# Later maxima and exps, an own copy of the second layer's first block, the values' bias with the attention's outputs, and another last step: one change with six parts to a two-layer kernel

## The chip, the cores and the metric

The kernel runs on one core of one Trainium2 chip. The metric is the time of one execution on the device in microseconds (us); the median of several executions counts. A core has a matrix engine (TensorE, in profiles PE, with weight loads as PEld), three engines for elementwise work (VectorE: DVE; ScalarE: ACT; GpSimd: POOL), and a sync engine (SP) that here only starts transfers. Each engine works through a queue of its own in the order written in the program, and waits on semaphores for the others. DMA transfers are started from the queues of SP, ACT and POOL.

## The reference

There are 8 batches of 512 rows and 512 features, all float32. Layer 0 is a graph attention: every row attends to the first 20 rows of its batch, in 16 heads and 2 directions, with a mask and an additive bias from 11 edge labels. Layer 1 is a self-attention over all 512 rows in 16 heads, with a layer norm before and after, scaled and shifted by gates computed from a condition vector.

```python
# layer 0; d = 0, 1 are the two directions of the edges
q_exp = where(x.sum(-1) == 0, 0, cond)                 # "live" rows
self_feat = concat([x, q_exp]) @ W_self.T + b_self
for d in range(2):
    aff = (self_feat @ Wq[d].T + bq[d]) . (self_feat[:, :20] @ Wk[d].T + bk[d]) / sqrt(32)
    aff = where(A[d].sum(-1) > 0, aff, -9e15) + A[d] @ w_bias + b_bias
    output += softmax(aff) @ self_feat[:, :20] @ Wout[d] + bout[d]
mid = x + relu(self_feat + output)
# layer 1
h = gamma * layernorm(mid) + beta                       # gamma, beta from cond
q, k, v = h @ Wqkv.T + bqkv
att = softmax(q . k) / sqrt(512)
h1 = (att @ v) @ Wp.T + bp + mid
out = gamma * layernorm(h1) + beta + h1
```

## The kernel before

**Start** (lines 169 to 385). SP loads, in this order, the near rows transposed and the first half of the self weights in four pairs of pieces (`vtk`, `ws`), batch 0 transposed (`vt`, four pieces), the condition's half of the self weights (`wc`), the near rows (`x_kv`, eight pieces) and batch 0 (`x`). PE computes the self features of the near rows (`psk`, 308), starts those of batch 0 (`psf`, 283), multiplies the condition by its weights (`pcw`, 253), and turns two sets of "live" flags (`pl`, 273) that DVE makes from row sums (`sums`, 265, needs `x`). Then come keys and output weights (`pk`, `pq`, `pw`). The values times output weights go to DRAM and are fetched per batch as block-diagonal tiles by `load_vo` (436 to 443, 20 transfers).

**Layer 0** (543 to 607) is a loop over 32 slots n = (b, c), a slot being 128 rows of batch b. It is a software pipeline written out by hand: slot n turns its own weights (`ptw`, 483), normalizes those of slot n+1 (`normalize0`: sum, reciprocal, POOL's multiply at 477), and computes the scores of slot n+2 (`scores0`, 454, with POOL's mask and bias at 460 and 461) and a quarter of the self features of the next batches (283 to 291). `exps0` (464 to 470) then subtracts the row's maximum (DVE 468, POOL 469) and takes the exp (ACT 470) of slot n+2. `result0` (488 to 497) sums self features and weighted values in `po`, DVE adds ReLU and x (496), and a store started from ACT's queue writes the block to `mid` in DRAM (497). Other work hangs at fixed slots: edge labels (`edges`, from 226), row sums of a later batch (`live_sums`), the second half of the keys (`keys(1, ..)`, n = 10 to 13), the gates' columns (`gates_t`, 515, n = 10). For layer 1, batch 0 is fetched back from `mid` at n = 23 (`fetch`, 97), its statistics are taken at n = 24, it is normed into `z` at n = 25 (108), turned at n = 26 and 27 (`turn`, 120), and the first queries, keys and values follow at n = 28 to 31. The same statistics and norm of batch 1 are at n = 29 and 30.

**Layer 1** (747 to 795) is a loop over 128 steps (b, group of 4 heads, 128 rows), again a pipeline by hand. In step n PE computes `scores(n+1)` (669), DVE the negated maxima (`tops`, 675), ACT the exps with their sums (681); `normalize` takes reciprocals on DVE (686) and scales on POOL (688); `turn_probs` transposes step n's probabilities (`pt`, 693) and ACT and DVE copy them (`et`, 695); `weigh` multiplies by the values (`pao`, 706), and ACT copies the result to `ao` (711 in the last batch, 713 before). Each step also holds half or all of one `Group` of four matmuls (133): queries, keys, values of the next batch, or the output projection (`ppj`) of the one before. A projection's `after` (643 to 646) adds the residual (645) and takes statistics (90 to 94); `finish` (648 to 656) applies norm and gates and stores the rows. The values' bias is multiplied by the output weights once and added to the output's bias (`value_bias`, 634 to 637, at step 2), since the probabilities of a row sum to a constant.

The last batch runs its steps in another order (664, row blocks outside), so that its own projections can start before all heads are done; `endings` (730) lists the projections of the last two batches, one half a step. In odd steps its `after` runs in the middle of the step, and a `finish` follows. Lines 796 to 802 are the tail: the last two `weigh`, and projection and `finish` of the last 128 rows.

Of the kernel before, what the change touches and what calls it, by code (L numbers as in the profile page):

```python
# [33 lines left out]


COLS = ["bk0", "bk1", "bq0", "bq1", "b_self", "b_q", "b_k", "b_v"]

# [5 lines left out]
@with_exitstack  # L43
def graph_then_self_attention(ctx: ExitStack, tc: tile.TileContext, x, x_t, near_t, cond_t, labels, w_self_t, wq, wk_t,
                              wout_t, wg_t, wb_t, wqkv_t, wp_t, cols, gate_vecs, rows, edge, out):
    nc = tc.nc
# [8 lines left out]
    make_identity(nc, ident)  # L55
    vec = const.tile([P, len(COLS), C], F32, name="vec")
    col = {name: vec[:, i, :] for i, name in enumerate(COLS)}
    edge_bc = const.tile([P, L + 1], F32, name="edge_bc")
    minus_half = const.tile([P, C], F32, name="minus_half")
# [40 lines left out]

    def norm_stats(b, c):
        statistics(XQ[b][:, c, :], f"{b}_{c}")

    def norm(b, c):
# [3 lines left out]
        nc.vector.tensor_scalar(Z[b][:, c, :], XQ[b][:, c, :], mv[:, 0:1], mv[:, 1:2], ALU.subtract, ALU.mult)  # L108

# [13 lines left out]
    class Group:  # L123
# [4 lines left out]

        def half(self, n):
            if n == 0:  # L130
                self.out = bank(self.name)
            for k in (2 * n, 2 * n + 1):
                nc.tensor.matmul(self.out, self.stationary(k), self.moving(k), start=(k == 0), stop=(k == C - 1))  # L133
            if n == 1:
                self.after(self.out)
# [17 lines left out]
    with ExitStack() as l0:  # L153
# [13 lines left out]


        vtk = three.tile([P, C, 2 * MH], F32, tag="t", name="vtk")
        ws = w0.tile([P, C, F], F32, name="ws")  # L170
        for k in range(C):
            nc.sync.dma_start(vtk[:, k, :], near_t[k * P:(k + 1) * P, :])
            nc.sync.dma_start(ws[:, k, :], w_self_t[k * P:(k + 1) * P, :])

        cond_sb = pro.tile([P, C, DH], F32, name="cond_sb")
        nc.vector.memset(cond_sb, 0.0)
        nc.scalar.dma_start(cond_sb[:, :, 0:B], blocks(cond_t))
        nc.scalar.dma_start(vec, cols.rearrange("p (k c) -> p k c", c=C))
        nc.scalar.dma_start(edge_bc, edge.partition_broadcast(P))

# [10 lines left out]
        def load_vt(b):  # L191
            VT[b] = turned.tile([P, C, N], F32, tag="turned", name=f"vt_{b}")
            for k in range(C) if b == 0 else (slice(0, C),):
                nc.sync.dma_start(VT[b][:, k], blocks(x_t[b])[:, k])

        load_vt(0)
        wc = weight("wc", w_self_t[F:2 * F, :])
        x_kv = wring.tile([MH, 2, F], F32, tag="w", name="x_kv")
        for i in range(2):
            for b in range(BH):  # L200
                nc.sync.dma_start(x_kv[NG * b:NG * (b + 1), i, :], x[BH * i + b, 0:NG, :])
        load_x(0)

        def room(name):
# [258 lines left out]

        def exps0(b, c):
            t = T[b, c]
            tv = t.rearrange("p h (d m) -> p (h d) m", d=2)
            top = three.tile([P, 2 * H, 1], F32, tag="top", name=f"top_{b}_{c}")
            nc.vector.tensor_reduce(top, tv, AX.X, ALU.max)  # L468
            nc.gpsimd.tensor_tensor(tv, tv, top.to_broadcast([P, 2 * H, NG]), ALU.subtract)  # L469
            nc.scalar.activation(tv, tv, AF.Exp)  # L470

        def normalize0(b, c):
            tv = T[b, c].rearrange("p h (d m) -> p (h d) m", d=2)
            den = three.tile([P, 2 * H, 1], F32, tag="den", name=f"den_{b}_{c}")
            nc.vector.tensor_reduce(den, tv, AX.X, ALU.add)  # L475
            nc.vector.reciprocal(den, den)  # L476
            nc.gpsimd.tensor_tensor(tv, tv, den.to_broadcast([P, 2 * H, NG]), ALU.mult)  # L477
# [55 lines left out]
        scores0(*slots[0])  # L533
        exps0(*slots[0])
        scores0(*slots[1])
        normalize0(*slots[0])
        exps0(*slots[1])
        for c in (0, 1):
# [4 lines left out]
        for n, (b, c) in enumerate(slots):  # L543
# [26 lines left out]
            if b + 1 + c // 2 < B:  # L570
                edges(b + 1 + c // 2, (c + 2) % 4)
# [57 lines left out]

    bv = w1.tile([P, C, P], F32, name="bv")  # L630

    def value_bias():

        pb = bank("pbv")
        for k in range(C):
            nc.tensor.matmul(pb, bv[:, k, :], wp[:, k, :], start=(k == 0), stop=(k == C - 1))
        nc.vector.tensor_tensor(bp_bc, pb, bp_bc, ALU.add)

# [10 lines left out]
    def finish(b, c):  # L649
# [47 lines left out]
    def weigh(n):  # L697
# [34 lines left out]

    with tc.manual_schedule():
        nc.sync.dma_start(bp_bc, rows[ROW_BP].partition_broadcast(P))
        fetch(2)
# [7 lines left out]
        for pair in range(2):  # L743
            normalize(0, pair)
        nc.vector.tensor_scalar(bv, col["b_v"].unsqueeze(2).to_broadcast([P, C, P]), att_scale, None, ALU.mult)

        for n, (b, g, c) in enumerate(steps):
# [53 lines left out]
        group.half(1)  # L801
        finish(B - 1, C - 1)

# [53 lines left out]
```

## Time and profile before

| | us |
|---|---|
| median of 3 runs (lowest, highest) | 1386.2 (1385.8, 1387.64) |
| the profiled execution | 1383.83 |
| its span, first to last instruction | 1382.0 |
| set-up, to the first slot of layer 0 | 80.4 |
| layer 0's slots, to layer 1 | 339.6 |
| layer 1 without its last batch | 859.0 |
| last batch and tail | 103.0 |

The mean clock granted to PE over the span is 0.995 of full speed. The four stretches are cut at 80.4, 420 and 1279 us of the span. All durations come from the one profiled execution; what an engine's "busy" leaves out are waits and the starting of transfers. A "releaser" is the instruction or transfer whose semaphore event ended an idle stretch. L477 stands for line 477 of the kernel before.

### The profile page before, as it was taken

How to read it: one execution, taken by the hardware profiler on the slowest of the kernel's cores; microseconds unless marked ns; L12 is line 12 of the kernel's file. 1: busy time of each engine (PE TensorE's matmuls, PEld its weight loads, DVE VectorE, ACT ScalarE, POOL GpSimd, SP SyncE). 2: the span in 40 equal slices, each digit the busy share in tenths (PEclk: the TensorE clock that was granted, in tenths of full speed). 3: DMA queues.
4: the chain of work that ended last, by engine and by line, in shares of the span. 5: the costliest groups of instructions: out<-in, count | busy, mean ns of one | idle time of the engine just before them, and what ended most of it. 6: DMA issues, size and time to landing. Idle time of an engine off the chain costs nothing.

```text
span 1382.0 us, 27718 instructions
## 1 busy us (share of the span) xinstructions
PE 1347.6 (98%) x10493; PEld 822.2 (59%) x10493; DVE 891.6 (65%) x1587; ACT 679.2 (49%) x1639; POOL 692.7 (50%) x807
## 2 busy tenths in 40 slices
PE   8999989999999999999999999999999999999997
PEld 5566666666665555655655555555556556555554
DVE  4566666666654456676577667657666765765786
ACT  1312122221125565655656666566566566566663
POOL 0255644556652345456355445545554553554655
PEclk9999999999999999999999999999999999999999
DMA  8624342344121000001001000100100010000001
GB/s 290 225 82 158 115 162 72 103 157 151 56 77 54 1 2 2 9 17 55 1 17 62 2 9 17 55 2 17 62 1 9 17 55 1 17 32 1 9 32 39
DMA packets 47043, 77.44 MB, mean 56 GB/s; under 512 B 10784, under 2 KB 15456, under 8 KB 46912
## 3 DMA queue, kind: packets, MB, share of 16 engines
q1 hardware_dynamic: 40976, 66.59, 14.2%
q10 hardware_dynamic: 5424, 8.43, 1.6%
q8 instruction: 85, 1.39, 0.4%
q0 software_dynamic: 512, 0.66, 0.2%
q14 instruction: 46, 0.38, 0.1%
HBM read 58.17 MB, written 17.49 MB: 55 GB/s over the span
## 4 chain that ended last, share of the span: by engine, by line
PE 78%; DVE 10%; POOL 6%; DMA 2%; issue 2%; SPq 1%; ACT 1%; ACTq 0%; POOLq 0%; DVEq 0%
PE pt L693 17%; PE pqk L133 15%; PE s L669 10%; PE pao L706 8%; PE pv L133 8%; PE ppj L133 8%; PE pss L454 4%; PE psf L283 3%; POOL t L460 2%; POOL t L461 2%; PE pw L423 1%; DVE top L468 1%; DVE sums L265 1%; DVE den L475 1%; PE pq L404 1%
## 5 line engine op out<-in xcount | busy, mean ns | idle before, releaser
L688 POOL TENSOR_SCALAR e<-e,den 128x512 f32<-128x512 f32 x512 | 374.6, 732 | 426.0 <-DVE den L686 387.1
L675 DVE TENSOR_REDUCE top<-s 128x2 f32<-128x1024 f32 x256 | 301.1, 1218 | 193.6 <-PE s L669 193.6
L681 ACT ACTIVATE e<-s,top 128x512 f32<-128x512 f32 x512 | 346.6, 701 | 11.9 <-DVE top L675 11.9
L693 PEld LDWEIGHTS pt<-ident,e 128*128 128x128 f32 x2048 | 229.4, 141 | 171.2 <-issue 90.0
L693 PE MATMUL pt<-ident,e 128*128 128x128 f32 x2048 | 274.1, 276 | 4.9 <-POOL e L688 4.6
L695 ACT COPY et<-pt 128x512 f32<-128x512 f32 x256 | 138.3, 589 | 235.0 <-PE pt L693 234.8
L133 PE MATMUL pqk<-ht,w 128*128 128x512 f32 x512 | 240.6, 593 | 0.0
L695 DVE COPY et<-pt 128x512 f32<-128x512 f32 x256 | 164.1, 683 | 0.0
L470 ACT ACTIVATE t<-t 128x640 f32<-128x640 f32 x32 | 23.6, 737 | 266.0 <-POOL t L469 266.0
L669 PE MATMUL s<-k,q 32*128 32x512 f32 x1024 | 147.4, 640 | 0.0
L454 PE MATMUL pss<-kq,sf 128*128 128x320 f32 x512 | 143.8, 434 | 0.0
L706 PEld LDWEIGHTS pao<-et,v 128*32 128x32 f32 x4096 | 107.7, 110 | 42.0 <-issue 40.8
L706 PE MATMUL pao<-et,v 128*32 128x128 f32 x4096 | 127.4, 274 | 0.6 <-ACT ao L711 0.4
L133 PEld LDWEIGHTS pqk<-ht,w 128*128 128x128 f32 x512 | 87.6, 190 | 62.5 <-issue 61.4
L133 PE MATMUL pv<-w,ht 128*128 128x512 f32 x256 | 120.9, 598 | 0.0
L133 PE MATMUL ppj<-w,ao 128*128 128x512 f32 x256 | 120.4, 593 | 0.0
L454 PEld LDWEIGHTS pss<-kq,sf 128*128 128x128 f32 x512 | 95.5, 191 | 36.5 <-issue 0.8
L283 PE MATMUL psf<-vt,ws 128*128 128x512 f32 x256 | 115.0, 593 | 0.0
L681 ACT ACTIVATION_READ_ACCUMULATOR e<-s,top 128x1 f32 x512 | 111.5, 218 | 0.0
L686 DVE RECIPROCAL den<-den 128x2 f32<-128x2 f32 x256 | 42.3, 165 | 84.2 <-ACT e L681 84.2
L477 POOL TENSOR_TENSOR t<-t,den 128x640 f32<-128x640 f32 x32 | 40.7, 1272 | 97.3 <-DVE den L476 87.0
L283 PEld LDWEIGHTS psf<-vt,ws 128*128 128x128 f32 x256 | 48.3, 190 | 50.7 <-issue 46.6
(186 smaller groups left out, 1351.9 us busy)
## 6 DMA issues: line engine op xcount, KB each, us to landing
x<-in_x SPq DMA_DIRECT2D x8, 1024.0 KB
mid<-x ACTq DMA_DIRECT2D x32, 256.0 KB
xq<-mid SPq DMA_DIRECT2D x8, 1024.0 KB
out<-o SPq DMA_DIRECT2D x32, 256.0 KB
vt<-in_x_t SPq DMA_DIRECT2D x7, 1024.0 KB
labels<-in_labels SPq DMA_DIRECT2D x16, 440.0 KB
wq<-in_wq SPq DMA_DIRECT2D x4, 1024.0 KB
gate<-gates SPq DMA_DIRECT2D x8, 512.0 KB
```

The costliest lines, as they stand in the source:

```text
L133: nc.tensor.matmul(self.out, self.stationary(k), self.moving(k), start=(k == 0), stop=(k == C - 1))
L283: nc.tensor.matmul(psf[f], ws[:, k, f * P:(f + 1) * P], VT[b][:, k, :], start=(k == 0), stop=(k == C - 1))
L454: nc.tensor.matmul(o, SF[b][:, k, cut], KQ[b][:, k, on], start=(k == 0), stop=(k == C - 1))
L477: nc.gpsimd.tensor_tensor(tv, tv, den.to_broadcast([P, 2 * H, NG]), ALU.mult)
L669: nc.tensor.matmul(S[n][j // 2][:, j % 2, :], Q[b, g][on, c * P:(c + 1) * P], K[b, g][on, :], start=True, stop=True)
L675: nc.vector.tensor_reduce(TOP[n][:, 2 * pair:2 * pair + 2], S[n][pair], AX.X, ALU.max, negate=True)
L681: nc.scalar.activation(e, S[n][j // 2][:, j % 2, :], AF.Exp, bias=TOP[n][:, j:j + 1], accum_out=DEN[n][:, j:j + 1])
L686: nc.vector.reciprocal(DEN[n][:, at], DEN[n][:, at])
L688: nc.gpsimd.tensor_scalar(E[n][j], E[n][j], DEN[n][:, j:j + 1], att_scale, ALU.mult, ALU.mult)
L693: nc.tensor.transpose(pt[:, k * P:(k + 1) * P], E[n][j][:, k * P:(k + 1) * P], ident)
L695: (nc.scalar.copy if j < 2 else nc.vector.tensor_copy)(et, pt.rearrange("p (k n) -> p k n", k=C))
L706: nc.tensor.matmul(PAO[b, g][DH * j:DH * (j + 1), at], V[b][:, k, DH * h:DH * (h + 1)], ET[n, j][:, k, :], start=(k == 0), stop=(k == C - 1))
```

## The change

Nothing in what is computed changes. The parts are:

- Layer 0: `exps0` is split. Maximum and subtraction (`less_top`) come after `result0` (in slots 26 to 29 still before it); the exp moves to the head of `normalize0`, in the next slot.
- The 32 stores to `mid` are started from SP's queue, in order with its loads, and no longer from ACT's.
- Start: `vtk` comes as one transfer from ACT's queue, `vt` of batch 0 in two, `x_kv` in one and after `x`; condition and edge weights come packed with the bias columns in one tile. Three matmuls on zeros stand ahead of PE's first work. `cond_r` is copied ahead of the sums of `x_kv`.
- Layer 1's first batch is normed from a copy of its own (`early`), loaded at n = 9; its statistics are spread over n = 15 to 18, its norm over 22 and 23; it is turned at n = 24 and 25, and its first groups are at n = 26, 27, 29 and 30. The last of the second layer's weights is loaded at n = 24 (before 20). Statistics and norm of batch 1 are one slot later, at 30 and 31.
- `value_bias` goes. ACT adds the scaled bias when it copies `pao` to `ao`.
- Last batch: `after` of a projection stands behind both reciprocals of the step; `finish` is in even steps. In the tail both `weigh` come first, and `finish_last` does the last 128 rows with two banks of 256 columns, statistics by halves, a side branch on POOL (`rest`) and two stores.

```diff
         vtk = three.tile([P, C, 2 * MH], F32, tag="t", name="vtk")
         ws = w0.tile([P, C, F], F32, name="ws")
+        nc.scalar.dma_start(vtk, near_t.rearrange("p (c m) -> p c m", c=C))
         for k in range(C):
-            nc.sync.dma_start(vtk[:, k, :], near_t[k * P:(k + 1) * P, :])
             nc.sync.dma_start(ws[:, k, :], w_self_t[k * P:(k + 1) * P, :])
-        cond_sb = pro.tile([P, C, DH], F32, name="cond_sb")
-        nc.vector.memset(cond_sb, 0.0)
-        nc.scalar.dma_start(cond_sb[:, :, 0:B], blocks(cond_t))
-        nc.scalar.dma_start(vec, cols.rearrange("p (k c) -> p k c", c=C))
-        nc.scalar.dma_start(edge_bc, edge.partition_broadcast(P))
+        nc.scalar.dma_start(vec, cols)
+        zeros = two.tile([P, N], F32, tag="live", name="zeros")[:, 0:2 * P]
+        nc.vector.memset(zeros, 0.0)
+        none = bank("none")
+        for i in range(3):
+            nc.tensor.matmul(none[:, 0:2 * P], zeros[:, 0:P], zeros, start=True, stop=True)
...
             VT[b] = turned.tile([P, C, N], F32, tag="turned", name=f"vt_{b}")
-            for k in range(C) if b == 0 else (slice(0, C),):
-                nc.sync.dma_start(VT[b][:, k], blocks(x_t[b])[:, k])
+            for cut in (slice(0, 2), slice(2, C)) if b == 0 else (slice(0, C),):
+                nc.sync.dma_start(VT[b][:, cut], blocks(x_t[b])[:, cut])
...
         x_kv = wring.tile([MH, 2, F], F32, tag="w", name="x_kv")
-        for i in range(2):
-            for b in range(BH):
-                nc.sync.dma_start(x_kv[NG * b:NG * (b + 1), i, :], x[BH * i + b, 0:NG, :])
         load_x(0)
+        nc.sync.dma_start(x_kv, near.rearrange("i m f -> m i f"))
...
         cond_r = two.tile([P, KB, P], F32, tag="wt", name="cond_r")[:, 0, :]
+        nc.vector.tensor_copy(cond_r, pcw[:, 2 * MH:2 * MH + P])
         nc.vector.tensor_reduce(sums_kv, x_kv, AX.X, ALU.add)
         nc.vector.tensor_scalar(sums_kv, sums_kv, 0.0, None, ALU.not_equal)
-        nc.vector.tensor_copy(cond_r, pcw[:, 2 * MH:2 * MH + P])
         live_sums(0)
...
-        def exps0(b, c):
+        def less_top(b, c):
             t = T[b, c]
...
             nc.gpsimd.tensor_tensor(tv, tv, top.to_broadcast([P, 2 * H, NG]), ALU.subtract)
-            nc.scalar.activation(tv, tv, AF.Exp)
         def normalize0(b, c):
+            nc.scalar.activation(T[b, c], T[b, c], AF.Exp)
             tv = T[b, c].rearrange("p h (d m) -> p (h d) m", d=2)
...
             nc.vector.scalar_tensor_tensor(X[b][:, c, :], po, 0.0, X[b][:, c, :], ALU.max, ALU.add)
-            nc.scalar.dma_start(mid[b, c * P:(c + 1) * P, :], X[b][:, c, :])
+            nc.sync.dma_start(mid[b, c * P:(c + 1) * P, :], X[b][:, c, :])
...
                 scores0(*slots[n + 2])
-            for i in range(2):
-                if i == 0 and b + 1 + c // 2 < B:
-                    self_feat(b + 1 + c // 2, ((c + 2) % 4,))
-                if i == 0 and n + 2 < len(slots):
-                    exps0(*slots[n + 2])
+            if b + 1 + c // 2 < B:
+                self_feat(b + 1 + c // 2, ((c + 2) % 4,))
+            if 26 <= n < len(slots) - 2:
+                less_top(*slots[n + 2])
             if c == 1 and b + 2 < B:
...
                 keys(1, n - 10, 0)
-            if n in (26, 27):
-                for f in (2 * (n - 26), 2 * (n - 26) + 1):
+            if n in (24, 25):
+                for f in (2 * (n - 24), 2 * (n - 24) + 1):
                     turn(0, f)
-            for i in {28: (0,), 29: (1,), 30: (2,), 31: (3,)}.get(n, ()):
+            for i in {26: (0,), 27: (1,), 29: (2,), 30: (3,)}.get(n, ()):
                 group = q_or_k(0, i, 0) if i < 2 else value(0, i - 2)
...
             result0(b, c)
+            if n < 26:
+                less_top(*slots[n + 2])
             if b + 1 + c // 2 < B:
...
-            if 17 <= n < 21:
-                W1.append(weight(f"w1_{n - 17}", (*(wqkv_t[i] for i in range(3)), wp_t)[n - 17]))
+            if n in (17, 18, 19, 24):
+                i = min(n - 17, 3)
+                W1.append(weight(f"w1_{i}", (*(wqkv_t[i] for i in range(3)), wp_t)[i]))
             if n in (23, 28):
                 fetch((n - 23) // 5)
-            if n == 24:
-                for i in range(C):
-                    norm_stats(0, i)
-            if n == 25:
-                for i in range(C):
-                    norm(0, i)
-            if n == 29:
+            if n == 9:
+                early = weight("early", mid[0])
+            if 15 <= n < 19:
+                norm_stats(0, n - 15, early)
+            for i in {22: (0, 1), 23: (2, 3)}.get(n, ()):
+                norm(0, i, early)
+            if n == 30:
                 for i in range(C):
                     norm_stats(1, i)
-            if n == 30:
+            if n == 31:
                 for i in range(C):
...
-    bv = w1.tile([P, C, P], F32, name="bv")
-    def value_bias():
-        pb = bank("pbv")
-        for k in range(C):
-            nc.tensor.matmul(pb, bv[:, k, :], wp[:, k, :], start=(k == 0), stop=(k == C - 1))
-        nc.vector.tensor_tensor(bp_bc, pb, bp_bc, ALU.add)
+    bv = w1.tile([P, C], F32, name="bv")
...
         nc.sync.dma_start(out[b, c * P:(c + 1) * P, :], o)
+    def finish_last():
+        b, c = B - 1, C - 1
+        h1, gate = XQ[b][:, c, :], GATE[b]
+        st = small.tile([P, 2, 6], F32, tag="st2", bufs=1, name="st_last")
+        mv = small.tile([P, 2], F32, tag="mv", name="mv_last")
+        o, rest = (op.tile([P, F], F32, tag="o", name=name) for name in ("o_last", "rest"))
+        out_p = [bank(f"ppj_last_{i}") for i in range(2)]
+        for i in range(2):
+            on = slice(i * F // 2, (i + 1) * F // 2)
+            for k in range(C):
+                nc.tensor.matmul(out_p[i][:, 0:F // 2], AO[b, k][:, c * P:(c + 1) * P], wp[:, k, on], start=(k == 0), stop=(k == C - 1))
+        for i in range(2):
+            on = slice(i * F // 2, (i + 1) * F // 2)
+            nc.vector.tensor_tensor(h1[:, on], out_p[i][:, 0:F // 2], h1[:, on], ALU.add)
+            nc.vector.bn_stats(st[:, i, :], h1[:, on])
+            nc.gpsimd.tensor_tensor(rest[:, on], h1[:, on], gate[:, 1, on], ALU.add)
+        nc.vector.bn_aggr(mv, st)
+        nc.vector.tensor_scalar(mv[:, 1:2], mv[:, 1:2], EPS, None, ALU.add)
+        nc.gpsimd.tensor_tensor(mv[:, 1:2], mv[:, 1:2], minus_half[:, 0:1], ALU.pow)
+        nc.vector.scalar_tensor_tensor(o, h1, mv[:, 0:1], gate[:, 0, :], ALU.subtract, ALU.mult)
+        for i in range(2):
+            on = slice(i * F // 2, (i + 1) * F // 2)
+            nc.vector.scalar_tensor_tensor(o[:, on], o[:, on], mv[:, 1:2], rest[:, on], ALU.mult, ALU.add)
+            (nc.scalar if i else nc.sync).dma_start(out[b, c * P:(c + 1) * P, on], o[:, on])
...
         if last:
-            nc.scalar.copy(AO[b, g][:, at], PAO[b, g][:, at])
+            nc.scalar.activation(AO[b, g][:, at], PAO[b, g][:, at], AF.Identity, bias=bv[:, g:g + 1])
         elif c == C - 1:
-            nc.scalar.copy(AO[b, g], PAO[b, g])
+            nc.scalar.activation(AO[b, g], PAO[b, g], AF.Identity, bias=bv[:, g:g + 1])
...
                 group.half(0)
-            elif b == B - 1:
-                ending[at // 2 - 1].half(at % 2)
+            elif b == B - 1 and more:
+                ending[at // 2 - 1].half(at % 2, take=False)
             if more:
...
                 finish(b - 1, (at - 3) // 2)
-            if b == B - 1 and at > 4 and at % 2:
-                finish(*endings[(at - 5) // 2])
+            if b == B - 1 and at > 2 and at % 2 and more:
+                ending[at // 2 - 1].after(ending[at // 2 - 1].out)
+            if b == B - 1 and at >= 4 and at % 2 == 0:
+                finish(*endings[at // 2 - 2])
             if group:
...
                 fetch(b + 2)
-            if n == 2:
-                value_bias()
             first = 0 if b == B - 1 else 10
...
                 bias(b, at - first)
+        ending[-1].half(1)
         weigh(len(steps) - 2)
+        weigh(len(steps) - 1)
         finish(*endings[-1])
-        weigh(len(steps) - 1)
-        group = project(B - 1, C - 1)
-        group.half(0)
-        group.half(1)
-        finish(B - 1, C - 1)
+        finish_last()
```

More of the change, by code (lines that the diff above doesn't have):

```diff
@@ L43, in graph_then_self_attention @@
 @with_exitstack
-def graph_then_self_attention(ctx: ExitStack, tc: tile.TileContext, x, x_t, near_t, cond_t, labels, w_self_t, wq, wk_t,
-                              wout_t, wg_t, wb_t, wqkv_t, wp_t, cols, gate_vecs, rows, edge, out):
+def graph_then_self_attention(ctx: ExitStack, tc: tile.TileContext, x, x_t, near, near_t, labels, w_self_t, wq, wk_t,
+                              wout_t, wg_t, wb_t, wqkv_t, wp_t, cols, gate_vecs, rows, out):
     nc = tc.nc
@@ L55, in graph_then_self_attention @@
     make_identity(nc, ident)
-    vec = const.tile([P, len(COLS), C], F32, name="vec")
-    col = {name: vec[:, i, :] for i, name in enumerate(COLS)}
-    edge_bc = const.tile([P, L + 1], F32, name="edge_bc")
+    nv = len(COLS) * C
+    vec = const.tile([P, nv + C * DH + L + 1], F32, name="vec")
+    col = {name: vec[:, i * C:(i + 1) * C] for i, name in enumerate(COLS)}
+    cond_sb = vec[:, nv:nv + C * DH].rearrange("p (c r) -> p c r", c=C)
+    edge_bc = vec[:, nv + C * DH:]
     minus_half = const.tile([P, C], F32, name="minus_half")
@@ L99, in fetch, with norm_stats, norm @@
         nc.sync.dma_start(XQ[b], blocks(mid[b]))
-    def norm_stats(b, c):
-        statistics(XQ[b][:, c, :], f"{b}_{c}")
-    def norm(b, c):
+    def norm_stats(b, c, src=None):
+        statistics((src or XQ[b])[:, c, :], f"{b}_{c}")
+    def norm(b, c, src=None):
         if c == 0:
@@ L107, in norm @@
         mv = STATS[f"{b}_{c}"]
-        nc.vector.tensor_scalar(Z[b][:, c, :], XQ[b][:, c, :], mv[:, 0:1], mv[:, 1:2], ALU.subtract, ALU.mult)
+        nc.vector.tensor_scalar(Z[b][:, c, :], (src or XQ[b])[:, c, :], mv[:, 0:1], mv[:, 1:2], ALU.subtract, ALU.mult)
     def bias(b, c):
@@ L127, in __init__, with half @@
             self.name, self.stationary, self.moving, self.after = name, stationary, moving, after
-        def half(self, n):
+        def half(self, n, take=True):
             if n == 0:
@@ L133, in half @@
                 nc.tensor.matmul(self.out, self.stationary(k), self.moving(k), start=(k == 0), stop=(k == C - 1))
-            if n == 1:
+            if n == 1 and take:
                 self.after(self.out)
@@ L533, in graph_then_self_attention @@
         scores0(*slots[0])
-        exps0(*slots[0])
+        less_top(*slots[0])
         scores0(*slots[1])
         normalize0(*slots[0])
-        exps0(*slots[1])
+        less_top(*slots[1])
         for c in (0, 1):
@@ L733, in graph_then_self_attention @@
     with tc.manual_schedule():
+        nc.vector.tensor_scalar(bv, col["b_v"], att_scale, None, ALU.mult)
         nc.sync.dma_start(bp_bc, rows[ROW_BP].partition_broadcast(P))
@@ L744, in graph_then_self_attention @@
             normalize(0, pair)
-        nc.vector.tensor_scalar(bv, col["b_v"].unsqueeze(2).to_broadcast([P, C, P]), att_scale, None, ALU.mult)
         for n, (b, g, c) in enumerate(steps):
@@ L826 @@
         gate_vecs[:, :B, i, :] = a[f"L1_cond_{name}"].reshape(4, 1, P)
+    cond = np.zeros((P, C, DH), np.float32)
+    cond[:, :, :B] = a["cond_1024"].reshape(B, C, P).transpose(2, 1, 0)
+    edge = np.tile(np.concatenate([a["L0_cond_w_bias"], a["L0_cond_b_bias"].reshape(1)]), (P, 1))
     arrays = {
@@ L829 @@
         "x_t": a["x"].transpose(0, 2, 1),
-        "near_t": a["x"][:, :NG].transpose(2, 0, 1).reshape(F, B * NG),
-        "cond_t": a["cond_1024"].T,
+        "near": a["x"][:, :NG].reshape(2, MH, F),
+        "near_t": a["x"][:, :NG].transpose(2, 0, 1).reshape(C, P, B * NG).transpose(1, 0, 2).reshape(P, C * B * NG),
         "labels": np.stack([adj[:, :, :NG], adj[:, :NG].transpose(0, 2, 1, 3)], axis=2).reshape(B, N, D2 * L),
@@ L840 @@
         "wp_t": a["L1_cond_Wp"].T,
-        "cols": np.concatenate([columns(vectors[name]) for name in COLS], axis=1),
+        "cols": np.concatenate([columns(vectors[name]) for name in COLS] + [cond.reshape(P, C * DH), edge], axis=1),
         "gate_vecs": gate_vecs.reshape(P, len(GATE_VECS), P),
         "rows": np.concatenate([a["L1_cond_bp"][None], a["L0_cond_bout"]], axis=0),
-        "edge": np.concatenate([a["L0_cond_w_bias"], a["L0_cond_b_bias"].reshape(1)]),
     }
```

## The prediction

> **What bounds it now.** I read the page's first section, then idle TensorE (PE) time by releaser (the waits view), then stretches (windows), then groups, the chain and a few timelines.
>
> ```profile
> PE   1347.6 (98%) x10493; PEld 822.2 (59%) x10493; DVE 891.6 (65%) x1587; ACT 679.2 (49%) x1639; POOL 692.7 (50%) x807
> 0.00:80.40 80.40, 73.88 (x523) 46.32 (x524) 37.76 (x100) 17.74 (x55) 20.86 (x32) 1.00 0.72 240
> 80.40:420.00 339.60, 325.52 (x1691) 221.36 (x1689) 212.71 (x429) 77.06 (x140) 185.09 (x144) 0.98 0.33 111
> 420.00:1279.00 859.00, 859.00 (x7376) 500.49 (x7376) 564.30 (x931) 528.86 (x1295) 426.53 (x559) 1.00 0.06 21
> 1279.00:1382.00 103.00, 89.16 (x906) 53.99 (x904) 76.83 (x129) 55.58 (x149) 60.24 (x74) 0.98 0.08 27
> ```
>
> The rows are set-up, layer 0's 32 slots, layer 1 without its last batch, and the last batch with the tail; columns: length, busy PE, PEld, DVE, ACT, POOL, clock. PE is the bound. From 420 to 1279 it never pauses, so there only removed PE work counts. Elsewhere it is idle 6.5 + 14.1 + 13.8 = 34.4 us, and some busy time is half-clock time. The idle time by cause:
>
> ```profile
> PE pt L693 <- POOL e L688: 4.6, 11, 0.5
> PE ptw L483 <- POOL t L477: 4.2, 4, 2.5
> PE pq L404 <- ACT gates_t L515: 4.2, 1, 4.2
> PE pz L120 <- DVE z L108: 2.5, 2, 2.2
> PE pq L404 <- ACT live L275: 1.5, 1, 1.5
> PE pl L273 <- DVE sfk L346: 1.3, 1, 1.3
> PE pcw L253 <- DMA wc<-in_w_self_t: 0.7, 1, 0.7
> ```
>
> (waiter, releaser: total, times, longest.) Each is a neighbour's queue order, not a lack of engine time. Timings below of single waits are the timeline's.
>
> **Layer 0, exps later.**
>
> ```profile
> L470 ACT ACTIVATE t<-t 128x640 f32<-128x640 f32 x32 | 23.6, 737 | 266.0 <-POOL t L469 266.0
> L477 POOL TENSOR_TENSOR t<-t,den 128x640 f32<-128x640 f32 x32 | 40.7, 1272 | 97.3 <-DVE den L476 87.0
> ```
>
> ACT stands 266 us in front of the exp, waiting for POOL's subtraction, with its copies of keys, gates and weights behind it. After the change the exp heads the next slot, its input ready one slot earlier. ACT's order becomes wt, exp, sf; DVE's x precedes the maximum, which idles 71.6 us on POOL today. No operation is added. Slots take 9.84 us (10.28 at c=1) without stalls; I charge the excess to its place:
> - n=5, 7, 9: .88 + .68 + .18; I take back 1.3.
> - n=10 to 13: 4.19 at the gates, then .4 + .4, then 1.46, plus a half-clock stretch of 3.41 us, which does half its work and so costs 1.7: 8.1. I keep .4 per slot, as key copies still fill these: 6.4 back.
> - n=25 to 27: .93, 2.18 + .33 and .11 + .59 of idle, 1.7 of half clock and about .5 of modelled ends: 6.3. Here also the early copy acts: z is made at n=22 and 23, two slots before its turn. The four statistics (.68+.18+.15 = 1.0 us DVE each) spread over n=15–18. 5.8 back.
> - n=30, 31: 2.49 + .4 idle, 1.7 of half clock: 4.6. DVE's 4.0 us of norm_stats(1) no longer stand ahead of den(31). But subtraction, exp .74, den 1.16 and multiply 1.27 for the last slot end about 6.6 us into slot 30, PE wants them at 5.5: 1.1 stays; the wt copy of .68, bare in slot 31, loses .4. 3.1 back.
>
> DVE at n=16 carries about 10.0 us for 9.84 (statistics, live sums of 2.2): I charge 1.0. Layer 0: 15.6 back; 10 if the new order stalls as often as half of the old, 18 if nothing stalls.
>
> The half-clock price is where rule and row differ. The Trainium skill, TensorE: Matmul & The Clock Gate, Why this matters for your kernels, asks for no idle gaps over about 3 us, since one idle window drops the clock. By that rule only the 4.19 gap costs clock, and the changes at n=26 and n=31 return 3.4 us less. The row speaks otherwise:
>
> ```profile
> 395.00:420.00 25.00, 22.51 (x93) 14.11 (x91) 12.64 (x27) 5.56 (x9) 11.18 (x11) 0.93 0.16 61
> ```
>
> After only 2.49 us of idle the matmuls from 412.69 to 416.11 ran at half rate; the same followed 2.18 + .33, while 1.46 and 1.27 cost no clock. I take the row.
>
> **mid on SP's queue.** 32 stores at .33 us of issue leave ACT, 10.6 us, none on the path. On SP they wait in order for x. Past them are moved: vo (20 issues) and labels behind mid(b,1), q_row behind mid(b,2), load_x behind mid(b,3), the next vt behind mid(b,0). load_x waited for that store already, vt and q_row are needed a slot or more later: nothing. vo and labels are the rival below. My value: 20 issues x .36 = 7.2, labels landing 3.7 later, so about 2.3 us into slot (b,3), against 5.7 before, since the 12 to 14 us that vo takes now include a wait for ACT's mid store. Zero cost; no gain counted.
>
> **Start.** x before x_kv, eight x_kv issues (8.29 us of SP) become one, constants in one DMA. x lands at 21.3 now and starts the chain sums 2.30, sfk, pl. Some 4.3 MB precede or are x; at the 320 to 400 GB/s of the DMA row from 10 us on it lands near 15. So .70 and 1.27 go. vtk as one 320 KB DMA beside ws may start PE .6 later. No row shows the three dummy matmuls: by psk's half-clock pace (.267 for 160 columns) 6 passes of 256 take 2.6 us. The same skill page and section ask for 4 us of continuous work before full speed, so by it 2.6 us and a gap bring nothing. The rows show full speed only at 9.92, 5.5 us after PE's first matmul, and all changes of clock on one grid of 3.41 us; work ahead of 4.41 can save one step, 1.7 us, or nothing (below nothing only by the .6). I take 1.3: together 3.3, range 1.4 to 4.
>
> **value_bias.**
>
> ```profile
> 450.63 3.43 PE pbv L636 x8
> ```
>
> The chain shows it with PE full: 3.43 goes, for certain. The bias on AO (28 + 16 ACT operations) makes 586 ns into about 688, the row of L141, same shape with a bias: +.10 each. ACT is busy 529 of 859, waits 35 us for pao; hidden. Uncovered, 28 x .10 = 2.9. w1_3 at n=24 is wanted 150 us later.
>
> **Last batch.** A pair of steps takes 12.87 us (1305.37 to 1318.24) for 11.38 of PE work; over 1293 to 1358 PE loses 8.3. The cause, from a timeline of an odd step:
>
> ```profile
> 1315.32 0.69 DVE L645 TENSOR_TENSOR xq<-ppj,xq 128x512 f32<-128x512 f32 x1 [0.74 <-PE ppj L133]
> 1316.05 0.69 DVE L90 BATCH_NORM_STATS2 st_h<-xq 128x6 f32<-128x512 f32 x1
> 1317.07 0.15 DVE L686 RECIPROCAL den<-den 128x2 f32<-128x2 f32 x1
> 1317.88 1.81 POOL L688 TENSOR_SCALAR e<-e,den 128x512 f32<-128x512 f32 x2
> 1318.62 0.55 PE L693 MATMUL pt<-ident,e 128*128 128x128 f32 x3 [0.38 <-POOL e L688]
> ```
>
> Addition and statistics (.69+.69+.18+.15 = 1.75 with gaps) stand before the reciprocal; POOL and PE wait for it. Moved behind both reciprocals, they leave the path, but DVE is then the loop: tops 2.35, reciprocals to about 3.0, et copies 1.28, second reciprocal .15, then 1.75 or finish's 1.5: 6.15 a step with gaps against PE's 5.69. Over 12 steps .46 each is 5.5, less 1.0 of slack: 4.5 lost instead of 8.3. 3.8 back; 0 if DVE's loop is as long as now, 7 if it overlaps fully, −3 if the longer-held ppj bank blocks the scores.
>
> **Tail.** From the last ppj (1373.6) addition, statistics, pow, two passes, POOL's gate and a DMA of 3.3 us run in line to 1382.0. Halves let .36 + .36 of DVE lie under PE, POOL's final 1.26 becomes a side branch, one pass lies under pow (1.0), the last pass and DMA are halved: about 2.3. The earlier last finish takes .74 passes and L655 out of the way: .8. 3.1, range 2 to 4.
>
> **Sum.** 15.6 + 3.3 + 3.4 + 3.8 + 3.1 = 29.2. The profiled execution took 1383.8 (span 1382.0 and 1.8 around it), 2.4 below the median of 1386.2. So span 1352.8, that execution 1354.6, median **1357**.
>
> **Rivals.**
> - Slower: labels. If vo needs its 14 us also behind mid(b,1), labels land 8.7 us into slot (b,3). DVE stands before edges, with t, den and x behind; POOL's multiply comes late, PE idles some 3.65 us and pays 1.7 of half clock: 5.3 for each of 6 batches, 32 in all: 1389. It decides from a landing about 5.1 us into the slot. For: DVE already waits 5.6 us for labels in four batches. Against: the cause of the long vo is gone. Chance .07, .02 of it for half of the batches.
> - Last batch: DVE becomes the bound at today's rate, 3.8 fewer: 1361. For: 6.15 above is near today's 6.43. Chance .16.
> - The start keeps its slow clock and late x, and layer 0 keeps its stalls in slots 30 and 31: 2 to 3 each: about 1363. Against: both have the order changed at their cause. Chance .13.
> - Better: stalls go with no rest, −5: 1352. It is in the forecast's case, which has .64.
>
> **Numbers.** Forecast's own range 1352 to 1361. 1350 to 1366 takes in the second and third rival and leaves the first, both misses together, and more than full gains. About 0.2% (2.8 us) is what a measurement tells from no change: faster .93, same .02, slower .05.
>
> **What would show it.** Right: the ACT idle behind L469 falls from 266 us to some tens; no clock drop after 100 us; no gates_t, z or live waits of PE; pbv absent; last-batch pairs near 12.3 us; PE busy about 1338 (1347.6 less 3.4 and 6.4 of half clock). Wrong: a PE wait through DVE edges for labels; dips of the clock at n=12 to 14, 26 or 31; xq statistics still ahead of PE's pt; PE start later than 5 us.

## The result and the profile after

The median fell from 1386.0 to 1360.9 us (4 runs each, 1360.13 to 1364.07 after), ratio 0.9823, interval 0.9804 to 0.9842. Forecast: 1357, range 1350 to 1366. The profiled execution after took 1364.07 (span 1362.3), the slowest of its four; that of before 1383.83, one of the fastest. So the two traces differ by 19.7 of span, the medians by 25.1; what is known of the difference is told below. First idle PE time after, by releaser:

```profile
PE ptw L486 <- POOL t L480: 3.1, 5, 1.7
PE pv L136 <- DVE x L499: 2.1, 1, 2.1
PE pq L407 <- DVE x L499: 1.6, 4, 0.4
...
PE pss L457 <- DVE kq L414: 1.0, 1, 1.0
PE pt L718 <- POOL e L713: 0.9, 2, 0.4
```

The waits for gates_t, live, z, sfk and wc are gone; `pt` waits 0.9 instead of 4.6. New are `pv` behind DVE's x, at the entry of layer 1, and `pss` behind a key copy. The exp's group shows the cause removed:

```profile
L475 ACT ACTIVATE t<-t 128x640 f32<-128x640 f32 x32 | 23.6, 737 | 78.1 <-POOL t L472 78.1
```

78 us of waiting instead of 266. Of the signs that the prediction named for being right, two did not come. PE is busy 1344.2 us and not about 1338, and the clock dropped after 100 us, at slot 31 (0.86 in the second row, 0.93 before):

```profile
PE 1344.2 (99%) x10499; PEld 823.7 (60%) x10499; DVE 907.2 (67%) x1589; ACT 687.5 (50%) x1639; POOL 692.2 (51%) x808
395.00:420.00 25.00, 20.73 (x82) 11.32 (x81) 12.69 (x28) 6.76 (x15) 8.28 (x11) 0.86 0.29 105
```

The stretches of the two traces, cut at the first instruction of the same work (gain in us):

| stretch | predicted | traces |
|---|---|---|
| start, to the first slot | 3.3 | 80.44 to 78.64: 1.8 |
| slots 0 to 13 | 7.7 | 163.38 to 154.77: 8.6 |
| slots 14 to 20 | −1.0 | 69.38 to 72.35: −3.0 |
| slot 21 to layer 1's first `pt` | 8.9 | 116.02 to 113.28: 2.7 |
| bias matmuls | 3.4 | 3.43 |
| last batch, to the last step's `pt` | 3.8 | 4.5 |
| tail | 3.1 | 1.6 |

The entry of layer 1 after, from the timeline (start, length, engine, line):

```profile
407.21 1.22 DVE L700 TENSOR_REDUCE top<-s 128x2 f32<-128x1024 f32 x1 [2.85 <-PE s L694]
408.35 0.14 DVE L96 TENSOR_SCALAR mv<-mv 128x1 f32<-128x1 f32 x1
408.41 0.68 DVE L499 SCALAR_TENSOR_TENSOR x<-po,x 128x512 f32<-128x512 f32 x1
```

```profile
401.45 0.76 PE L486 MATMUL ptw<-ident,t 128*128 128x128 f32 x5 [1.72 <-POOL t L480]
402.05 0.60 PE L496 MATMUL po<-ident,sf 128*128 128x128 f32 x4
403.05 2.50 PE L498 MATMUL po<-vo,wt 128*128 128x128 f32 x10 [0.40 <-ACT wt L488]
405.49 1.60 PE L694 MATMUL s<-k,q 32*128 32x512 f32 x8
409.24 4.94 PE L136 MATMUL pv<-w,ht 128*128 128x512 f32 x7 [2.15 <-DVE x L499]
```

In the instruction stream DVE has layer 1's first maximum (`top`) ahead of x of slot 31, though the source has it behind: where the two hand-ordered regions meet, their instructions were merged. DVE stands in front of `top` until the scores end, x waits behind it, and PE's `pv` waits for the bank that x frees. The pauses of 1.72 + 0.40 and of 2.15 us each brought a stretch of 3413 ns at half clock (403.06 and 409.89): `po` takes 2.50 instead of 1.28.

### The profile page after: what moved, and what is told of

It reads as the page before. It is cut to its first block, busy times and chain, and to the rows that moved or that the text cites. A ratio compares the mean times of both kernels' runs of the same rounds, so it can differ in the third digit from the quotient of the medians.

```text
span 1362.3 us, 27708 instructions
## 1 busy us (share of the span) xinstructions
PE 1344.2 (99%) x10499; PEld 823.7 (60%) x10499; DVE 907.2 (67%) x1589; ACT 687.5 (50%) x1639; POOL 692.2 (51%) x808
## 4 chain that ended last, share of the span: by engine, by line
PE 93%; DVE 4%; POOL 2%; issue 0%; DMA 0%; ACT 0%; POOLq 0%; DVEq 0%; ACTq 0%
PE pt L718 18%; PE pqk L136 16%; PE s L694 10%; PE pao L731 9%; PE pss L457 8%; PE ppj L136 8%; PE pv L136 8%; PE psf L286 7%; PE po L498 2%; PE pw L426 1%; PE ptw L486 1%; PE pz L123 1%; PE pq L407 1%; PE po L496 1%; POOL t L464 1%; POOL t L463 1%
## 5 line engine op out<-in xcount | busy, mean ns | idle before, releaser
L136 PE MATMUL ppj<-w,ao 128*128 128x512 f32 x248 | 116.7, 593 | 0.0
L488 ACT COPY wt<-ptw 128x640 f32<-128x640 f32 x32 | 22.2, 693 | 108.0 <-PE ptw L486 107.6
```

## The experiments

Time is the median of 4 runs (5 in the last), ratio that of the run to the kernel before on the same chip, with its interval. "After" is 1360.9. The kernel before itself took 1384.3 to 1386.0 on the chips of these runs, so a difference of under some 2 us between medians of different chips says little by itself; there the traces decide. "Excess" is what a slot takes over 9.84 us, or over 10.28 in each batch's second slot.

**Exps early again.** Maximum, subtraction and exp in one place as before (the exp goes from the head of `normalize0` to the end of `less_top`):

```diff
-            nc.scalar.activation(T[b, c], T[b, c], AF.Exp)
+            nc.scalar.activation(tv, tv, AF.Exp)
-            if 26 <= n < len(slots) - 2:
+            if n < len(slots) - 2:
```

> The changed kernel (1360.9 us) with layer 0's maximum, subtraction and exp back at their old place, all else changed. Theory: the later exps carry most of layer 0's gain; PE's waits for gates_t (about 4 us, with a half-clock stretch of 1.7), live (1.5) and the POOL multiply come back, 8 to 11 us: 1369 to 1372. At the same time DVE's mask comparison (L239), which takes 0.84 us in the changed kernel and 0.24 before, falls back to about 0.24, because it no longer runs beside POOL's subtraction. Rival: the gain of layer 0 comes from the own copy of the first block and from mid leaving ACT's queue; then this costs under 3 us (1361 to 1364), and the gates_t wait stays away.

Measured 1374.1 (0.9920, 0.9905 to 0.9935): 13.2 more. The waits are back:

```profile
PE pq L407 <- ACT gates_t L518: 4.2, 1, 4.2
...
PE pq L407 <- ACT live L278: 1.4, 1, 1.4
```

Slot 14 starts 10.9 us later than after. The mask comparison takes 0.18 to 0.24 again. Theory held; its size (8 to 11) was low. In this trace the pause at the gates brought two half-clock stretches, 6.83 us, where one had been counted.

**First blocks as before.** No `early`; statistics, norm, turn and groups at their old slots.

> The changed kernel (1360.9 us) with the second layer's first blocks as before: no own copy, statistics at slot 24, norm at 25, turn at 26 and 27, groups at 28 to 31, batch 1 at 29 and 30. Theory: the z wait of 2.2 + 0.3 us and its half-clock stretch (1.7) return, but what the change paid for it goes: the POOL waits of slots 17 to 21 (about 2.6) and the stall at the entry of layer 1 (2.15, a wait for x of slot 31, and its half clock of 1.7); net within 2 us: 1359 to 1363. Rival, the prediction's sum: this part earned 5.8 of layer 0's gain and nothing is paid for it elsewhere: 1366 to 1367.

Measured 1365.7 (0.9860, 0.9845 to 0.9875): 4.8 more, between the two. In the traces slots 17 to 22 are free of excess (10.28 and 9.84), which is 2.7 back, and z (2.2 + 0.3) and a `ptw` of 3.2 return:

```profile
PE ptw L486 <- POOL t L480: 5.9, 4, 3.2
PE pz L123 <- DVE z L111: 2.5, 2, 2.2
```

With each half-clock stretch taken off at 1.7, slot 24 to the first `pt` of layer 1 takes 84.4 against 79.0: there the part earned 5.4, and it paid 2.7 in slots 17 to 22. That nets 2.7 of the median's 4.8. The rest was not traced; the mean clocks of the single runs (0.996 to 0.998 here, 0.996 to 1.000 after) allow for more half-clock stretches here.

**Last batch and tail as before.**

> The changed kernel (1360.9 us) with the last batch's steps and the tail as before. Theory: 4.5 us of the last batch and 1.6 of the tail return, 6.1 in all: 1367, with pairs of steps at 12.9 us again instead of 11.9. Rival: the pair time is set by ACT's 14 operations and not by DVE's order, so that only the tail's part returns: 1362 to 1363.

Measured 1367.8 (0.9879, 0.9864 to 0.9894): 6.9 more; from step 112 to the end 114.1 against 108.0 in the traces, 6.1 as expected, pairs 12.88 against 12.09, and PE's waits are those of before:

```profile
PE pt L718 <- POOL e L713: 4.6, 11, 0.5
```

**Bias matmuls back.** `value_bias` at step 2, AO copied without a bias.

> The changed kernel (1360.9 us) with the eight bias matmuls back and AO copied without bias. Theory: PE has no idle time where they stand, so all of 3.43 us returns: 1364.3, with nothing else moved (the copies of pao with a bias, 0.1 us dearer each, are covered). Rival: the dearer copies cost something in the last batch, where ACT and DVE are near their limit; then less than 2.5 returns.

Measured 1365.6 (0.9864, 0.9848 to 0.9881): 4.7 more. Between steps 0 and 8 the traces differ by 3.44, elsewhere in layer 1 by under 0.2. The rest of the median's difference was not traced; the drops of the clock told below differ from run to run by more.

**mid from ACT's queue.**

```diff
-            nc.sync.dma_start(mid[b, c * P:(c + 1) * P, :], X[b][:, c, :])
+            nc.scalar.dma_start(mid[b, c * P:(c + 1) * P, :], X[b][:, c, :])
```

> The changed kernel (1360.9 us) with the 32 stores of mid started from ACT's queue again. Theory: the store's issue of 0.33 us is covered on either queue, labels land in time on either: within 1.5 us of 1360.9. Rival: behind the x of its slot the store holds ACT's wt copy and exp of the next slot; slots grow by 0.3 us or more, 5 to 10 us slower: 1366 to 1371.

Measured 1358.8 (0.9812, 0.9797 to 0.9827): 2.1 faster, which neither expected. The slots are unchanged but for 0.2 us at slots 5 and 6 and 0.5 at slot 30: the stores themselves give the change nearly nothing. The merge at the joint came out otherwise: x of slot 31 stands ahead of `top`, the `pv` wait is absent, and no clock drop follows.

**Labels ahead of the maximum.**

```diff
-            if n < 26:
-                less_top(*slots[n + 2])
             if b + 1 + c // 2 < B:
                 edges(b + 1 + c // 2, (c + 2) % 4)
+            if n < 26:
+                less_top(*slots[n + 2])
```

> The changed kernel (1360.9 us) with the edge labels ahead of maximum and subtraction in slots below 26: the same instructions in another order on DVE. Theory: the mask comparison waited for the end of POOL's subtraction on a path both share (0.84 against 0.24 us, ending at the same moment as the subtraction); apart from it, it takes 0.24, DVE gains 0.6 us a slot, and the excess of slots 14 to 21 (about 3.5 us over 9.84 and 10.28) falls to under 1.5: 1358 to 1359. Rival: that excess comes from the statistics moved into these slots and from row sums alone; then the time stays within 1 us of 1360.9, also if the mask takes 0.24.

Measured 1364.5 (0.9856, 0.9837 to 0.9874), 3.6 slower, where 2 to 3 faster was expected. Slots 14 and 17 to 21 lost 2.6 of their excess, but slots 3, 7 and 23 gained 3.3, where DVE now waits for labels ahead of the maximum:

```profile
DVE total L238 <- DMA labels<-in_labels: 9.4, 5, 2.6
```

After, that wait is 0.6. The single runs differ by 6 us, so the median's 3.6 is not all told by the slots' 0.7. This is the labels' lateness of the slower rival; the order of the change itself keeps it off the path.

**One order over both layers**, opened once ahead of layer 0, in place of one for each layer:

```diff
+    ctx.enter_context(tc.manual_schedule())
...
-        l0.enter_context(tc.manual_schedule())
...
-    with tc.manual_schedule():
```

> The changed kernel (1360.9 us) with both layers under one hand-written order. In the changed kernel's instruction streams DVE has the first maximum of layer 1 ahead of x of slot 31, though the source has it behind; here it is behind, PE's order is the same. Theory: PE's wait of 2.15 us for that x goes, with the half-clock stretch after it (1.7): 2 to 4 us faster, 1357 to 1359. Rival: the wait only moves, since the norm of batch 1 (2 us of DVE) then stands ahead of layer 1's first maxima and PE waits for the first probabilities: within 1 us of 1360.9.

Measured 1358.5 (0.9811, 0.9796 to 0.9826): 2.4 faster; span 1356.4, no clock drop between 9.7 us and the end. Layer 1's first `pt` comes 12.1 us after slot 31 began; after it is 17.6: 2.1 for the wait, 3.4 for two half-clock stretches. Theory held for the wait. The clock of the same window is 1.00, where it is 0.86 after:

```profile
395.00:420.00 25.00, 22.88 (x108) 12.26 (x106) 15.85 (x33) 11.02 (x26) 10.73 (x15) 1.00 0.30 105
```

That no drop came at all is in part chance: the pauses of 1.72 and 0.40 of slot 31 stay, and of the four kernels below, which have this order too, two still dropped behind them, the one with the mask comparison last for two stretches and the one with the moved finish for one.

**Nine matmuls on zeros.**

> The changed kernel (1360.9 us) with nine matmuls on zeros ahead of the first work in place of three. Theory: the clock rises only after a whole stretch of 3.41 us of the grid with PE busy throughout; three matmuls leave a pause of 0.6 us ahead of psk, so the rise came at 10.5 us. Nine take up to 8.8 us at half clock, so PE is busy without a pause from 1.2 us, the clock rises between 4.6 and 8.0 us, and psk starts late, 6 to 9 us: the two about cancel, 0.5 faster to 2.5 slower, and the profile shows the rise at 8 us or before. Rival: the clock rises with the first work of real data and not by the zeros; then the rise stays past 10 us and the time is some 4 us longer, 1365.

Measured 1361.5 (0.9831, 0.9815 to 0.9847), 0.6 slower. The clock rose at 5.1 us, PE being busy from 1.2 on; `psk` began at 7.1. First slot at 78.08 against 78.64. The size held. That a stretch must be busy throughout did not: in the bias run the clock rose behind one with 14% of idle.

**Four matmuls, near rows ahead of x** (on top of one order, 1358.5, as the next two):

```diff
-        for i in range(3):
+        for i in range(4):
...
+        nc.sync.dma_start(x_kv, near.rearrange("i m f -> m i f"))
         load_x(0)
-        nc.sync.dma_start(x_kv, near.rearrange("i m f -> m i f"))
```

> The kernel with both layers under one order (1358.5 us, first slot at 78.3 us), with four matmuls on zeros in place of three, and the near rows (still one transfer) ahead of x. Theory: four fill PE without a pause from 1.2 to 4.7 us, so the clock rises at 8.0 us at the latest; and the start is bound by the row sums that follow the last of the two transfers, 1.2 + 2.3 us of DVE after 17.4; with the near rows first, 1.2 of it lies under x's landing. First slot at 76.8 to 77.5, time 1357 to 1358. Rival: what lands last bounds the start and not the order, the first slot stays at 78 or later, also with an early rise of the clock: 1358 to 1359.

Measured 1356.5 (0.9786, 0.9770 to 0.9803), 2.0 faster; first slot at 76.68. Two things changed here, but other traces tell them apart: in ten with three matmuls and the near rows behind x the first slot lies at 77.68 to 78.74, whether the clock rose at 4.04 or at 10.68, and with nine matmuls at 78.08. So most of the gain is the order.

**Mask comparison last.**

> The kernel with both layers under one order (1358.5 us), with the mask comparison as the last of the label instructions, behind POOL's subtraction in time; the maximum stays ahead of the labels. Theory: the comparison takes 0.24 or less in nearly all slots, DVE gains 0.6 us a slot without a wait for labels ahead of the maximum, and slots 14 and 17 to 21 lose some 2 to 3 us of their excess: 1355.5 to 1356.5. Rival: another instruction takes over the wait for POOL (the addition of the edge weight, same form), DVE gains nothing: 1358 to 1359.

Measured 1358.1 (0.9800, 0.9783 to 0.9817), 0.4 faster, within the noise: the slots are the same to 0.05 us. The mask takes 0.18, but the multiplication of the labels, now next to the subtraction, grew:

```profile
L239 DVE TENSOR_TENSOR labels<-labels,vec 128x440 f32<-128x440 int32 x32 | 36.1, 1128 | 1.1
```

It was 0.60. The theory fell and the rival held: the wait for POOL only moved, and what sets the pace had to be sought in the order of both engines.

**Finish of step 126 moved** behind the last copies of probabilities.

> The kernel with both layers under one order (1358.5 us), with the finish of step 126 moved behind the last copies of probabilities. Theory: its two passes on DVE (0.93 and 0.99 us there, 0.74 elsewhere) and POOL's scaling of the last probabilities (0.91 each, 0.76 elsewhere) slow each other; apart, POOL's four take 3.05 instead of 3.66, PE's two waits of 0.44 go, and the end comes 0.6 to 0.9 us sooner: 1357.6 to 1357.9. Rival: the moved finish only delays the one behind it and the last pass on DVE: no gain, 1358 to 1359.

Measured 1357.8 (0.9796, 0.9781 to 0.9811), 0.7 faster, about the noise; the trace is clear: POOL's four take 3.04, PE's waits are gone, the passes take .74 and .75; from the last step's `pt` to the end 17.2 against 17.8.

**All that helped, statistics ahead of the maximum.**

```diff
+            if 15 <= n < 19:
+                norm_stats(0, n - 15, early)
             if n < 26:
                 less_top(*slots[n + 2])
```

> The changed kernel (1360.9 us) with both layers under one order, four matmuls on zeros and the near rows ahead of x, the finish of step 126 moved, and the statistics of slots 15 to 18 ahead of the maximum in place of behind the labels. Theory: in slots 18 and 19 of the changed kernel a loop over two engines sets the pace: maximum .82, labels 3.0, statistics 1.0, sum and reciprocal 1.2 on DVE, then multiply 1.27, mask 1.54 and addition 1.54 on POOL, with hand-overs 10.34 us against PE's 9.84; DVE meanwhile stands 2.6 us ahead of each maximum. Statistics in that pause leave the loop, 9.3: slots 17 to 21 lose 2 of their 2.6 us of excess. With 1.7 of the start and 0.5 of the tail over 1358.5: 1354 to 1355. Rival: the statistics do not come apart from the loop, and slots 17 to 21 keep their excess: 1356 to 1357.

Measured 1353.9 (1353.24 to 1357.87; 0.9787, 0.9771 to 0.9804): 7.0 faster than after. Slots 17 to 21 take 10.44, 9.90, 9.84, 9.84 and 10.28 instead of 10.95, 10.33, 10.35, 9.90 and 11.17, and of PE's five waits for POOL's multiply one is left, at slot 31:

```profile
PE ptw L486 <- POOL t L480: 1.7, 1, 1.7
```

The other edits act at the start, the joint and the tail, so in these slots it was the place of the statistics, as the loop had it. Slot 14 keeps its 1.3. The windows of layer 0's slots (length, busy PE, PEld, DVE, ACT, POOL, clock) show clock 1.00 throughout:

```profile
76.60:405.00 328.40, 323.67 (x1709) 219.85 (x1708) 232.18 (x433) 80.33 (x141) 184.86 (x144) 1.00 0.36 119
```

## Why the prediction was right, point by point

**Right in mechanism and size.** Exps later: slots 0 to 13 gave 8.6 for 7.7, and undoing them costs 13.2. The early copy: slots 24 to 29 went from 61.05 to 57.36 with one group more in them (before, the four groups are in slots 28 to 31, after in 26, 27, 29 and 30). A group takes 3.43 (slot 27 with one 9.84, slot 28 without 6.41), so this gave 7.1 for 5.8; with the first blocks as before these slots take 60.99. Bias: 3.43, with copies at 688 ns as priced. The DVE loop of the last batch was foretold at 6.15 us a step; a pair takes 12.09, 6.05 each (6.16 for the step shown, 5.93 for the one ahead of it):

```profile
1316.42 2.35 DVE L700 TENSOR_REDUCE top<-s 128x2 f32<-128x1024 f32 x2
1319.21 0.17 DVE L711 RECIPROCAL den<-den 128x2 f32<-128x2 f32 x1 [0.45 <-ACT e L706]
1319.29 1.27 DVE L720 COPY et<-pt 128x512 f32<-128x512 f32 x2
1320.55 0.17 DVE L711 RECIPROCAL den<-den 128x2 f32<-128x2 f32 x1
1320.63 0.93 DVE L652 SCALAR_TENSOR_TENSOR o<-xq,mv_h,gate 128x512 f32<-128x512 f32 x1
1321.66 0.99 DVE L653 SCALAR_TENSOR_TENSOR o<-o,mv_h,xq 128x512 f32<-128x512 f32 x1
1322.58 2.34 DVE L700 TENSOR_REDUCE top<-s 128x2 f32<-128x1024 f32 x2
```

DVE idles 0.45 us a step here, for ACT's exps, so the loop runs through both; PE's row says busy without a break: a busy PE was not a PE at its peak. The labels did not decide: DVE waits 0.6 us for them.

**Slots 30 and 31: 3.1 foretold as gain, 3.4 lost.** From slot 30 to layer 1's first `pt` both traces take 25.01, but the one after has a group less in it, 3.43. Before, 2.49 of idle and 1.7 of half clock were lost there (the 0.4 of idle that the prediction adds is no wait of PE in that trace); after, 1.72, 0.40 and 2.15 of idle and twice 1.7. So the residual of slot 31 was there, 1.72 for 1.1, and the 0.4 for wt too. What failed is "1.1 stays" as the whole price: the 2.15 of the joint was missing from it, though the merge could be read in the instruction streams, and I let the half-clock stretch there go, though 1.72 + .40 of idle in one stretch of 3.41 were enough. That is a part of the spread between traces and medians: how two pauses fall on the clock's grid differs from run to run. The traces of the change and of the five experiments that keep its joint (exps, last batch, bias, labels, nine matmuls) show two, one, none, one, two and one drop there, 0 to 3.4 us. The row of the profile that the prediction took was the right base for this, not the rule of the Trainium skill (TensorE: Matmul & The Clock Gate, Why this matters for your kernels, gaps of about 3 us): pauses of 2.12 in one stretch and of 2.15 in another dropped the clock, each 62 or 63% of its stretch.

**DVE in slots 14 to 20: 1.0 charged, 3.0 paid.** "About 10.0 us for 9.84" was DVE's sum alone. The pace was a loop through two engines. Slot 18 after, from one maximum to the next:

```profile
278.27 0.82 DVE L471 TENSOR_REDUCE top<-t 128x32 f32<-128x640 f32 x1 [2.62 <-POOL t L464]
281.84 0.69 DVE L93 BATCH_NORM_STATS2 st<-early 128x6 f32<-128x512 f32 x1
282.85 0.81 DVE L478 TENSOR_REDUCE den<-t 128x32 f32<-128x640 f32 x1
284.19 1.27 POOL L480 TENSOR_TENSOR t<-t,den 128x640 f32<-128x640 f32 x1 [0.62 <-DVE den L479]
285.42 1.54 POOL L463 TENSOR_TENSOR t<-t,mask 128x640 f32<-128x640 f32 x1
287.04 1.54 POOL L464 TENSOR_TENSOR t<-t,add 128x640 f32<-128x640 f32 x1
288.61 0.82 DVE L471 TENSOR_REDUCE top<-t 128x32 f32<-128x640 f32 x1 [2.63 <-POOL t L464]
```

10.34 us go round, DVE standing 2.6 ahead of the maximum with the statistics (`st`) behind it. It costs 0.5 to 0.7 in slots 17 to 19 and 0.9 in 21; 1.3 more is slot 14, where key copies stand behind labels; that one is no part of the loop, and the run without the early copy has it too. A part of the loop is the mask comparison, 0.84 instead of 0.24, which ends with POOL's subtraction:

```profile
246.25 1.27 POOL L472 TENSOR_TENSOR t<-t,top 128x640 f32<-128x640 f32 x1 [2.29 <-DVE top L471]
246.72 0.84 DVE L239 TENSOR_SCALAR mask<-total 128x40 f32<-128x40 f32 x1
```

The Trainium skill (GPSIMD Engine Reference, 1. Specifications) says that POOL shares its way to the local memory with DVE's two-input and two-port instructions; the runs agree: comparison and two-input multiplication waited (0.24 to 0.84, 0.60 to 1.27), the reductions did not (0.60 in both orders). Whether the comparison, which has one input, runs in a two-port mode no run here shows. Moving the subtraction next to the labels brought this wait about.

**Start: 3.3 foretold, 1.8.** The waits went (1.97), the 1.3 for the clock did not come: three matmuls leave a pause of 0.6 ahead of `psk`, and the rise came at 10.53. In the run with the bias matmuls back it came at 4.5, and the first slot still at 78.4, PE now waiting 1.8 for `sums_kv`: the row sums after the last transfer set the end, and x_kv behind x made that later: it landed at 17.4 us, where the prediction had x near 15. The 4 us of continuous work that the prediction set against the matmuls were not needed: in the labels run the clock rose 2.8 us after PE's first matmul.

**Tail: 3.1 foretold, 1.6.** From PE's end to the last store 6.2 instead of 8.4, 2.2 as foretold. The 0.8 for the earlier finish turned into a loss: beside it POOL's four scalings took 3.66 instead of 3.05, and moving it away gave 0.5 back.

**Sum.** In the traces the misses are −1.5, −2.0, −6.2 and −1.5, and +0.9 and +0.7: 19.7 for 29.2. The median gained 25.1, since the profiled execution after lies 3.2 above its median and that of before 2.2 below. The two drops at the joint are 3.4 of it at most; the rest of that difference stays open. That the median came within 4 us of the forecast is in part luck: the early copy and the exps gave 2.2 more than foretold, and the joint cost clock in some executions only.

## What to carry to other kernels

Where work is moved into slots that seem free, add up the loop through all engines that hand to each other, not one engine's sum; put the added work into the pause in which that engine stands waiting. Read the instruction streams at every place where two orders meet. A residual stall priced by its length alone is too cheap where the clock follows it.

## What the runs showed of the hardware

PE's clock rose only behind a stretch of the 3.41 us grid with little pause, and no clean bound shows: with 14% and 17% of the stretch idle it rose (4.48 and 4.04 us, bias and labels runs), with 16% and 18% it did not, and rose a stretch later (9.15 last batch, 10.53 after). Nor does one for the fall: behind stretches with 2.12, 1.90 (moved finish) and 1.78 us (mask comparison last) of idle it fell, behind 1.97 (first blocks as before) and 1.86 (last batch as before) it did not.

Some instructions of POOL and DVE slow each other in both directions. Beside each other in the last step, DVE's two passes took 0.93 and 0.99 us and two of POOL's scalings 1.01 each (after); with the finish moved away, 0.74, 0.75 and 0.69. Their ends alternate (POOL 1345.20, DVE 1345.73, POOL 1346.29, DVE 1346.83, POOL 1347.39), as if one at a time got through; that reading is inferred.
